# Twenty node tiles of layer 3 kept in SBUF for layer 4, and seven subtractions of the prologue moved to GpSimd

## The chip, the cores and the metric

The kernel runs on one core of one Trainium2 chip. The metric is the device time of one execution in microseconds (us). A core has TensorE (PE, matrix products), VectorE (DVE), ScalarE (ACT), GpSimd (POOL) and SyncE (SP), and 16 DMA engines that carry transfers between HBM and SBUF for all of them. Each engine works through its own queue in order. A DMA is started by an instruction in the queue of SP, ACT or POOL; rows that are picked by an index list ("gathers") are started by POOL.

## The reference, cut to what matters

A four-layer graph network over 6250 nodes with 256 features and 100,000 edges, sorted by destination. With `h = relu(layernorm(x))`:

```python
msum = segment_sum(h[src], dst)                       # layer 1: mean
h = h @ W1_self + (msum / clip(deg, 1)) @ W1_neigh + b1
hp = relu(h @ W2_pool + b2_pool)                      # layer 2: max
h = h @ W2_self + segment_max(hp[src], dst) @ W2_neigh + b2
h = ((segment_sum(h[src], dst) + h) / (deg + 1)) @ W3_neigh + b3   # layer 3
h = h @ W4_self + (segment_sum(h[src], dst) / clip(deg, 1)) @ W4_neigh + b4
out = x + (h @ W_fc + b_fc)                           # layer 4 and the end
```

Destinations are drawn as `6250 * u**2`, so low node numbers have many incoming edges and high ones few.

## The kernel before, in words

**Tiles.** The nodes are cut into 49 tiles of 128 (NT = 49). A table of rows in HBM holds what a layer needs of every node: `tab_h` in layer 1, `tab_r` in layer 3, `tab_s` in layer 4. Weight products are folded together, so that a node's row in `tab_s` is 256 numbers for the neighbours' sum of layer 4, kept as a high and a low part (2 x 256 fp32r, 2 KB a row, 256 KB a tile), while the node's own part goes to the table `xq`.

**Two ways to sum over neighbours.** For the low node tiles (8 in layer 1, H3 = 20 in layer 3, H4 = 22 in layer 4) the sum is dense: a matrix of edge counts, held in `tab_a` as fp8, times the rows of all 49 tiles, one PE instruction for each pair of a destination and a source tile (function `dense`). For the other node tiles the function `sums` walks over the edges, 128 at a time: POOL gathers 128 rows into one of `deep` slots of `ring` (14 in layer 4), DVE makes a one-hot matrix `hot`, PE multiplies them, and DVE adds the product to `acc`. The dense products stand in a list, the `Hub`; `sums` works it off beside the gathers, so many of the list at each step that the list ends 8 steps before the gathers in layer 4. PE's order in layers 3 and 4 is thus: the products in front of the first step, then one product of a gather and some four dense ones, in turn.

**Layer 3's end of a node tile.** `done3` (lines 1834 to 1868) turns an accumulator into `q`, splits its second half with `halves` (ACT copies the high part, DVE subtracts for the low part) into `q2`, and SP stores `q2` to `tab_s` and the first half to `xq`. For the 20 dense tiles a first part of the sum, made during layer 2, is added: it lies in the 20 tiles `acc3_0` to `acc3_19` of 2 KB a partition, in the pool `span3`, which closes with layer 3. For tiles 33 to 42 (`z4_kept`) `q2` is not a passing buffer: it lies in `zt33` and `zt38` of the pool `zk`, which lives through layer 4.

**Layer 4** (lines 1870 to 1940). It has 22 x 49 = 1078 dense products, 266 gathers and 266 products of gathers. The source tiles come in the order of `order`: first the ten kept ones, then six groups of `z4_late`, which `resident` loads back from `tab_s` on SP's queue. For the first four destination tiles the products go group by group, so that 4 x 10 = 40 of them need no load; `hub.advance(4 * nk)` puts these 40 ahead of the first gather's step. The count matrices come in pieces `ac` on ACT's queue, nine pieces ahead, and ACT widens each to `af`. The working pool `fl4` lies where layer 3's pool `fl3` was. `done4` and `finish4` load x (`xr`) and `xq` (`q`) on ACT's queue, add the sums on DVE, and store `out` on SP's queue.

**The prologue** (lines 660 to 1108). The x rows come in 17 groups of three tiles (the last has one). For each group DVE takes mean and variance (L706 to L714), ACT the root (L715), DVE the inverse and the shift `nb` (L721, L729), ACT normalizes (L731) and casts the high part to bf16 in `Z1` (L733), DVE subtracts it (`middle`, L737), POOL casts the middle part (L739), DVE subtracts again for the lowest part (`lowest`, L743), and SP stores the group to `tab_h` (L745). DVE's order is written out by hand: `lowest` of group g-1 stands inside the statistics of group g+2. A planner orders the other engines, save where `keep_in_program_order` pins an instruction behind the one traced before it on its engine. Five buffers `xt` hold the groups; the load of group g+4 is written behind `lowest` of group g-1, whose buffer it takes, and stands behind its store in SP's queue. POOL also issues five gathers (`begins`, L806) in groups 0 and 1 and two (`window_gathers`, L872) in each of groups 5 to 12.

Of the kernel before, what the change touches and what calls it, by code (L numbers as in the profile page):

```python
# [9 lines left out]
F32 = mybir.dt.float32  # L10
# [3 lines left out]
F32R = mybir.dt.float32r  # L14
# [7 lines left out]
P = 128  # L22
# [56 lines left out]
def fast_path(  # L79
# [15 lines left out]
    nc = tc.nc  # L95
    N, FI = x.shape
    E = src.shape[0]
    FH = W1_self.shape[1]
    FO = W_fc.shape[1]
    NT = (N + P - 1) // P  # L100
# [7 lines left out]
    LG = 7  # L108
# [7 lines left out]
    for d in range(NT):  # L116
        m, s = _edges_below(d * P, E, N)
        m1, s1 = _edges_below((d + 1) * P, E, N)
# [9 lines left out]
    for d in range(NT):  # L128
        m, s = _edges_below(d * P, E, N)
        m1, s1 = _edges_below((d + 1) * P, E, N)  # L130
# [7 lines left out]
    H1, H3, H4 = HUB  # L138
# [502 lines left out]
    Z1 = zpool.tile([P, NT, 3 * FI + 4], BF16, name="Z1")  # L641
# [21 lines left out]
    with ExitStack() as pro:  # L663
# [6 lines left out]
        xts = []  # L670
# [69 lines left out]

        def lowest(g):
            i0, LG = groups[g]
            nc.vector.tensor_sub(Z1[:, i0 : i0 + LG, 2 * FI : 3 * FI], xts[g],  # L743
                                 Z1[:, i0 : i0 + LG, FI : 2 * FI])
            nc.sync.dma_start(  # L745
                tab_h[i0 * P : (i0 + LG) * P, :].rearrange("(c p) f -> p c f", p=P),
                Z1[:, i0 : i0 + LG, :],
            )
# [110 lines left out]
        nk = max(RB1, RB * P - RB1)  # L859
# [239 lines left out]
    with ExitStack() as on:  # L1099
# [91 lines left out]
        hub = Hub(made.rest() + work)  # L1191
# [105 lines left out]
    nc.scalar.dma_start(srcE, stash_e[0, :, jb - JC * P : T - JC * P].bitcast(I32))  # L1297
    keyE = span4.tile([P, T - jb], F32, name="keyE")
    nc.scalar.dma_start(keyE, stash_e[1, :, jb - JC * P : T - JC * P])
    acc3 = [span3.tile([P, FH], F32, name=f"acc3_{d}") for d in range(H3)]  # L1300
    begun = set()

    def add3(d, v):
# [517 lines left out]
    with ExitStack() as on:  # L1821
        psd = on.enter_context(tc.tile_pool(name="psd3", bufs=2, space=PSUM))
        psg = on.enter_context(tc.tile_pool(name="psg3", bufs=3, space=PSUM))
        psm = on.enter_context(tc.tile_pool(name="psm3", bufs=2, space=PSUM))
        one_tag[id(psm)] = "pm"
        zk = on.enter_context(tc.tile_pool(name="fz4", bufs=1, side="right"))
        Z4 = {}
        z4_kept = ((33, 38), (38, 43))
        z4_late = ((0, 7), (7, 14), (14, 20), (20, 27), (27, 33), (43, NT))
        for s0, s1 in z4_kept:  # L1830
            zt = zk.tile([P, s1 - s0, 2 * FO], F32R, name=f"zt{s0}", bufs=1)
            Z4.update({s: zt[:, s - s0, :] for s in range(s0, s1)})

        with tc.tile_pool(name="fl3", bufs=2) as wk:
            def done3(d, acc):
                q = wk.tile([P, FH], F32, name="q", bufs=2)
                if d < H3:
                    nc.vector.tensor_add(q, acc, acc3[d])
                    nc.vector.scalar_tensor_tensor(q, q, rgcn[:, d : d + 1], qrow,
                                                   op0=ALU.mult, op1=ALU.add)  # L1840
                else:
                    if d in Z3:
                        z = Z3[d]
                    else:
                        z = wk.tile([P, 3 * FH], BF16, name="zown", bufs=1)
                        with tc.issue_after(kept_stores[-1].ins):
                            nc.sync.dma_start(z, tab_r[d * P : (d + 1) * P, :])
                        yield 1
                        yield 1
                        yield 1  # L1850
                    if d < NT - 4:
                        for part in range(3):
                            nc.vector.tensor_add(acc, acc, z[:, part * FH : (part + 1) * FH])
                            yield 1
                    else:
                        own = bank(psm, "pm", "pm_own")
                        for part in range(3):
                            nc.tensor.matmul(own, ident_b, z[:, part * FH : (part + 1) * FH],
                                             start=(part == 0), stop=(part == 2))
                        yield 1  # L1860
                        nc.vector.tensor_add(acc, acc, own)
                    nc.vector.scalar_tensor_tensor(q, acc, rgcn[:, d : d + 1], qrow,
                                                   op0=ALU.mult, op1=ALU.add)
                q2 = Z4[d] if d in Z4 else wk.tile([P, 2 * FO], F32R, name="q2")
                halves(q[:, FO:], FO, q2)
                nc.sync.dma_start(tab_s[d * P : (d + 1) * P, :], q2.bitcast(F32))
                nc.sync.dma_start(xq[d * P : (d + 1) * P, :], q[:, :FO])
                yield 1

            late = ((0, 4), (4, KEPT), (EARLY[1], 45), (45, NT))  # L1870
            Z3 = {s: kept_rows[0][:, s, :] for s in range(KEPT)}
            with tc.issue_after(kept_stores[-1].ins):
                for s0, s1 in ((EARLY[1], NT),):
                    Z3.update(resident(wk, tab_r, FH, s0, s1))
            block = stream(wk, [(d, s0, s1) for d in range(H3) for s0, s1 in late], wk,
                           lambda s: s < KEPT)
            todo = []
            work = []
            for d in range(H3):
                work += dense([s for s0, s1 in late for s in range(s0, s1)], lambda s, d=d: block(d, s), lambda s: Z3[s], FH, psd,  # L1880
                              lambda acc, d=d: todo.append(done3(d, acc)), own=d,
                              halved=range(KEPT))
            sums(wk, psg, tab_r, FH, srcE, keyE, jb, H3, done3, 11, Hub(work), wait=14, todo=todo,
                 rest=12)

        upto3.close()
        settle(zk, on.enter_context(tc.tile_pool(name="flp", bufs=1, space=PSUM)))
        with tc.tile_pool(name="fl4", bufs=2) as wk:
            loaded4 = {}

            def load4(d):
                n = P if d < NFULL else NREM
                xr = wk.tile([P, FI], F32, name="xr4", bufs=10)
                nc.scalar.dma_start(xr[:n, :], x[d * P : d * P + n, :])
                q = wk.tile([P, FO], F32, name="q4", bufs=10)
                nc.scalar.dma_start(q[:n, :], xq[d * P : d * P + n, :])
                loaded4[d] = n, xr, q

            def done4(d, acc):
                for i in range(d, min(d + 3, H4 if d < H4 else NT)):  # L1900
                    if i not in loaded4:
                        load4(i)
                return finish4(d, acc)

            def finish4(d, acc):
                n, xr, q = loaded4.pop(d)
                yield 1
                yield 1
                yield 1
                nc.vector.tensor_add(xr[:n, :], xr[:n, :], q[:n, :])  # L1910
                for c in range(0, acc.shape[1], FO):
                    nc.vector.scalar_tensor_tensor(xr[:n, :], acc[:n, c : c + FO],
                                                   rmean[:n, d : d + 1], xr[:n, :],
                                                   op0=ALU.mult, op1=ALU.add)
                nc.sync.dma_start(out[d * P : d * P + n, :], xr[:n, :])

            order = [*z4_kept, *z4_late]
            first = range(4)
            block = stream(zk, [(d, *c) for c in order for d in first]
                           + [(d, *c) for d in range(4, H4) for c in order],  # L1920
                           wk, deep=9, ahead=4)
            todo = []
            parts4 = []
            for d in range(H4):
                parts4.append(dense([s for s0, s1 in order for s in range(s0, s1)],
                                    lambda s, d=d: block(d, s), lambda s: Z4[s], FO, (psd, psm)[d // 2 % 2],
                                    lambda acc, d=d: todo.append(done4(d, acc)), wide=True))
            nk = sum(s1 - s0 for s0, s1 in z4_kept)
            cuts = [sum(s1 - s0 for s0, s1 in order[:i]) for i in range(len(order) + 1)]
            hub = Hub([w for a, b in zip(cuts, cuts[1:]) for d in first for w in parts4[d][a:b]]  # L1930
                      + [w for p in parts4[4:] for w in p])
            hub.advance(4 * nk)
            for s0, s1 in z4_late:
                Z4.update(resident(wk, tab_s, FO, s0, s1))
            sums(wk, psg, tab_s, FO, srcE, keyE, jb, H4, done4, 14, hub, wait=4, todo=todo,
                 rest=8, wide=True)
# [643 lines left out]
```

## Time and profile before

| what | value |
|---|---|
| median of 3 runs | 2724.58 us (2719.38 to 2725.16) |
| the profiled execution | 2732.06 us, its span 2730.3 us |
| prologue, to the first gather of layer 1 | to about 113 us |
| layer 3 | about 1960 to 2360 us |
| layer 4, from its first product to the end | 2360.8 us to the end |
| busy over the span: PE, DVE, POOL, ACT | 84%, 76%, 68%, 48% |

The profile comes from one execution. A timeline row gives start and duration in us, engine (SPq and ACTq are queues that issue DMAs), line, operation, and in square brackets how long the engine was idle before, and what ended that. A row of stretches gives the stretch, its length, the busy time of each engine with the number of its instructions, the granted TensorE clock as a share of full speed, the mean busy share of the 16 DMA engines, and what they moved in GB/s.

### The profile page before, as it was taken

The page shows a single profiled execution, that of the slowest core. Times are in us where ns is not written, and L with a number is a line of the kernel's source. Part 1 is how long each engine was busy: PE and PEld are TensorE (multiplying, and loading weights), DVE is VectorE, ACT ScalarE, POOL GpSimd, SP SyncE. Part 2 cuts the span into 40 slices and gives each one's busy share as a digit, 9 for nine tenths or more (in the row PEclk, how much of TensorE's full clock was granted, in tenths as well). Part 3 has the DMA queues.
Part 4 walks back from the last instruction along what each step waited for, and adds up shares of the span by engine and source line. Part 5 has one row for each costly group of instructions (what it writes and reads, how often), then busy time and mean ns, then how long its engine had stood idle before and what let it go on. Part 6 is the DMA issues. An engine that isn't in the chain of part 4 may idle for free.

```text
span 2730.3 us, 37722 instructions
## 1 busy us (share of the span) xinstructions
PE 2303.3 (84%) x10402; PEld 1436.1 (53%) x10402; DVE 2084.6 (76%) x5540; ACT 1301.6 (48%) x2859; POOL 1858.7 (68%) x2169
## 2 busy tenths in 40 slices
PE   4688999999787366566978999898799999879987
PEld 2356666777443132222645666655345445568766
DVE  8888777776489898888678998888467777557666
ACT  4467777764278888696422333232211111234443
POOL 5477777777567677677656676566477777667775
PEclk8799999999898578778989999999899999989999
DMA  8567777777699899899989999999799999999996
GB/s 272 157 178 206 209 206 212 217 222 232 200 356 341 295 343 346 290 322 358 342 288 305 339 343 318 283 321 311 283 380 385 378 383 363 333 364 351 315 302 216
DMA packets 365625, 809.90 MB, mean 297 GB/s; under 512 B 56238, under 2 KB 154646, under 8 KB 365372
## 3 DMA queue, kind: packets, MB, share of 16 engines
q0 software_dynamic: 143248, 501.86, 56.3%
q1 hardware_dynamic: 145928, 215.57, 21.7%
q10 hardware_dynamic: 76228, 89.96, 9.7%
q8 instruction: 85, 1.39, 0.2%
q14 instruction: 136, 1.11, 0.1%
HBM read 602.51 MB, written 205.46 MB: 296 GB/s over the span
## 4 chain that ended last, share of the span: by engine, by line
PE 49%; DMA 26%; DVE 13%; issue 5%; ACT 2%; POOL 2%; ACTq 0%; DVEq 0%; POOLq 0%; SPq 0%
PE pd L574 18%; PE pg L513 11%; DMA X<-rows,srcIf 9%; DMA ring<-tab_h,srcT 4%; DVE run L1669 3%; PE pm_hp L1175 3%; PE pm_prf L1558 3%; DMA rows<-X 2%; DMA xr<-in_x 2%; PE pm_hp L1169 2%; PE pb L349 2%; DVE acc L544 2%; DVE X L1669 2%; DMA out<-xr 2%; PE pm_prf L1552 2%
## 5 line engine op out<-in xcount | busy, mean ns | idle before, releaser
L1688 POOL DMA_INDIRECT X<-rows,srcIf x782 | 744.5, 952 | 368.0 <-issue 143.8
L1669 DVE SCALAR_TENSOR_TENSOR run<-run,samef,X 128x512 f32<-128x512 f32 x758 | 573.1, 756 | 52.8 <-DMA X<-rows,srcIf 47.1
L492 POOL DMA_INDIRECT ring<-tab_h,srcT x474 | 456.7, 963 | 150.1 <-issue 53.2
L513 PE MATMUL pg<-ring,hot 128*128 128x259 bf16 (+1 forms) x2292 | 475.1, 316 | 45.9 <-DMA ring<-tab_h,srcT 34.8
L544 DVE SCALAR_TENSOR_TENSOR acc<-pg,M,acc 128x256 f32<-128x256 f32 (+2 forms) x617 | 314.6, 536 | 79.5 <-PE pg L513 71.1
L492 POOL DMA_INDIRECT ring<-tab_r,srcE x290 | 292.1, 1007 | 117.1 <-issue 51.8
L1794 ACT CAST af<-ac 128x768 fp32r<-128x768 fp8e4 (+3 forms) x216 | 172.7, 805 | 384.7 <-DMA ac<-tab_a 193.4
L513 PEld LDWEIGHTS <-hot 128*128 128x128 bf16 x2292 | 214.0, 98 | 231.6 <-issue 108.7
L492 POOL DMA_INDIRECT ring<-tab_s,srcE x266 | 255.4, 960 | 110.5 <-PE pg L510 34.8
L566 PE MATMUL pd<-zt,af 128*128 128x512 f32 x1078 | 300.7, 402 | 33.5 <-ACT af L1794 30.5
L1669 DVE SCALAR_TENSOR_TENSOR X<-X,samef,run 128x512 f32<-128x512 f32 x379 | 282.3, 745 | 38.1 <-DMA X<-rows,srcIf 23.1
L574 PE MATMUL pd<-kept_rows,aw 128*128 128x512 f32 x920 | 293.9, 443 | 12.7 <-ACT aw L1624 6.5
L566 PEld LDWEIGHTS pd<-zt,af 128*128 128x128 f32 x1078 | 207.3, 194 | 86.2 <-ACT af L1794 38.9
L574 PEld LDWEIGHTS pd<-kept_rows,aw 128*128 128x128 f32 x920 | 175.8, 194 | 85.1 <-issue 35.3
L488 DVE TENSOR_SCALAR hot<-iota_bf,keyE 128x128 bf16<-128x128 bf16 (+1 forms) x556 | 143.9, 281 | 82.8 <-PE pg L513 51.9
L1558 PE MATMUL pm_prf<-unf,hTf 128*128 128x512 f32 x384 | 201.3, 649 | 1.9 <-ACT hTf L1548 1.3
L341 ACT ACTIVATE hs<-ht,onef 128x128 bf16<-128x128 bf16 x396 | 153.5, 393 | 90.6 <-PE pb L349 89.5
L1624 ACT CAST aw<-ae 128x512 fp32r<-128x512 fp8e4 x160 | 99.2, 621 | 188.0 <-PE pd L574 173.4
L574 PE MATMUL pd<-Z,A 128*128 128x256 bf16 (+1 forms) x1176 | 184.1, 273 | 0.8 <-ACT A L354 0.7
L375 ACT ACTIVATE ht<-iota_bf,skR 128x128 bf16<-128x128 bf16 x448 | 157.9, 402 | 12.8 <-DMA col<-in_L_gnn_b 8.9
L340 ACT ACTIVATE ht<-iota_bf,sk 128x128 bf16<-128x128 bf16 x396 | 153.1, 398 | 8.3
L393 PE MATMUL pb<-hm,hs 128*128 128x196 bf16 x448 | 82.2, 282 | 87.9 <-ACT A L398 77.5
(391 smaller groups left out, 4184.1 us busy)
## 6 DMA issues: line engine op xcount, KB each, us to landing
rows<-X SPq DMA_DIRECT2D x385, 256.0 KB, 4.8
tab_r<-r ACTq DMA_DIRECT2D x48, 384.0 KB, 4.7
rows<-hpf SPq DMA_DIRECT2D x49, 256.0 KB, 3.6
th<-tab_t ACTq DMA_DIRECT2D x49, 256.0 KB, 6.1
X<-rows,srcIf POOLq DMA_INDIRECT x782
tab_a<-A ACTq DMA_DIRECT2D x14, 784.0 KB, 6.6
ae<-tab_a SPq DMA_DIRECT2D x160, 64.0 KB, 4.9
tab_s<-q SPq DMA_DIRECT2D x39, 256.0 KB, 6.9
```

What stands on the lines that cost most here:

```text
L340: nc.scalar.activation(t, iota_b, AF.Abs, bias=sk[:, r : r + 1])
L341: nc.scalar.activation(hots[0], t, AF.Relu, bias=one, scale=-1.0)
L375: nc.scalar.activation(held["ht"][:, i, :], iota_b, AF.Abs, bias=sk[:, r : r + 1])
L492: nc.gpsimd.indirect_dma_start(out=ring[:, j % deep, :].bitcast(F32) if wide else ring[:, j % deep, :], out_offset=None, in_=table, in_off ...
L513: mm = nc.tensor.matmul(pg[:, : F + c], hot[j], X[:, part * F : (part + 1) * F + c], start=(k == 0 and part == 2), stop=(k == n - 1 and pa ...
L544: nc.vector.scalar_tensor_tensor(acc[d], half, m, acc[d], op0=ALU.mult, op1=ALU.add)
L566: nc.tensor.matmul(hold[0], a, z, start=(s == ss[0]), stop=(s == ss[-1]))
L574: nc.tensor.matmul(hold[0][:, : F + c], a, z[:, part * F : (part + 1) * F + c], start=(first and s != own), stop=(s == ss[-1] and part == ...
L1558: nc.tensor.matmul(pm, hT[:, c, :], un[:, c, :], start=False, stop=(c == KH - 1))
L1669: nc.vector.scalar_tensor_tensor(put, held, st, row, op0=ALU.mult, op1=ALU.max)
L1688: nc.gpsimd.indirect_dma_start(out=X[:, k, :], out_offset=None, in_=tab_p, in_offset=bass.IndirectOffsetOnAxis(ap=srcI[:, t : t + 1], axis=0),
L1794: nc.scalar.copy(wide[i][:, :n, :], got[i][:, :n, :])
```

## The change

1. The tiles `acc3_0` to `acc3_19` move from the pool `span3` to `span4`, which lives through layer 4. When `done3` of a dense tile d has read `acc3_d`, its `q2` is written to a new tile in the same place, `z4_d`. It is still stored to `tab_s`, since gathers read any row.
2. In layer 4 the source order starts with tiles 0 to 19, then the ten kept ones, then those that are loaded: 20 to 26, 27 to 32 and 43 to 48. Three loads (tiles 0 to 19) are gone, and 4 x 20 = 80 products instead of 40 stand ahead of the first gather's step.
3. In the prologue `lowest` of the odd groups 1 to 13 (seven of 17) runs on POOL; all 17 are pinned in program order. On POOL each stands behind the cast and the gathers of its own group and ahead of the cast of the next.

```diff
         def lowest(g):
             i0, LG = groups[g]
-            nc.vector.tensor_sub(Z1[:, i0 : i0 + LG, 2 * FI : 3 * FI], xts[g],
-                                 Z1[:, i0 : i0 + LG, FI : 2 * FI])
+            by = nc.gpsimd if g % 2 and g < 14 else nc.vector
+            tc.keep_in_program_order(
+                by.tensor_sub(Z1[:, i0 : i0 + LG, 2 * FI : 3 * FI], xts[g],
+                              Z1[:, i0 : i0 + LG, FI : 2 * FI]))
...
-    acc3 = [span3.tile([P, FH], F32, name=f"acc3_{d}") for d in range(H3)]
+    acc3 = [span4.tile([P, FH], F32, tag=f"acc3_{d}", name=f"acc3_{d}", bufs=1) for d in range(H3)]
...
+        z4_first = ((0, 7), (7, 14), (14, H3))
         z4_kept = ((33, 38), (38, 43))
-        z4_late = ((0, 7), (7, 14), (14, 20), (20, 27), (27, 33), (43, NT))
+        z4_late = ((H3, 27), (27, 33), (43, NT))
...
+                if d < H3:
+                    Z4[d] = span4.tile([P, 2 * FO], F32R, tag=f"acc3_{d}", name=f"z4_{d}", bufs=1)
                 q2 = Z4[d] if d in Z4 else wk.tile([P, 2 * FO], F32R, name="q2")
...
-            order = [*z4_kept, *z4_late]
+            order = [*z4_first, *z4_kept, *z4_late]
...
-            nk = sum(s1 - s0 for s0, s1 in z4_kept)
...
-            hub.advance(4 * nk)
+            hub.advance(4 * H3)
```

## The prediction, made before the changed kernel was run

> **What bounds the kernel now.** I read the stretches first, then the chain of waits, then the timelines of PE and POOL where layer 4 starts, and the same for the prologue. The change touches only these two places, so only they are priced. Stretches of layer 4 (columns: stretch, length, PE, PEld, DVE, ACT, POOL busy with counts, PE clock, DMA share, GB/s):
>
> ```profile
> 2360.00:2380.00 20.00, 19.16 (x73) 15.19 (x74) 6.22 (x24) 10.85 (x14) 14.60 (x16) 0.86 0.95 348
> 2380.00:2400.00 20.00, 13.36 (x51) 10.32 (x50) 4.76 (x14) 4.36 (x5) 15.12 (x17) 0.91 1.04 409
> 2400.00:2420.00 20.00, 8.57 (x28) 6.00 (x28) 3.20 (x10) 2.94 (x4) 6.22 (x7) 0.67 1.04 390
> 2450.00:2500.00 50.00, 50.00 (x221) 41.23 (x220) 37.37 (x119) 23.65 (x29) 38.12 (x40) 1.00 1.02 354
> 2600.00:2650.00 50.00, 42.92 (x174) 33.10 (x175) 30.25 (x94) 20.33 (x24) 38.03 (x40) 0.97 0.93 301
> ```
>
> In steady work PE does 221 products in 50 us, 0.226 us each. From 2380 to 2420 it does 79, where 177 would fit: PE starves for 22 us, its clock falls to 0.67, and the DMA engines are full. The chain says on what:
>
> ```profile
> 2375.13 33.04 DMA zt<-tab_s
> ```
>
> These are the reloads of layer 3's rows, which the change halves. The last PE hole ends at 2418.09, behind them; PE's first 40 products, of the kept tiles, had taken 11.8 us:
>
> ```profile
> 2360.84 11.80 PE L566 MATMUL pd<-zt,af 128*128 128x512 f32 x40 [5.63 <-ACT af L1794]
> ...
> 2418.09 1.22 PE L566 MATMUL pd<-zt,af 128*128 128x512 f32 x2 [8.80 <-ACT af L1794]
> ```
>
> But PE's holes are not yet the kernel's loss. The gathers on POOL are a second pacer: one every 1.25 us, 266 of them. In the timeline of POOL, and in the view of all instructions on `tab_s`:
>
> ```profile
> 2360.83 0.94 POOL L492 DMA_INDIRECT ring<-tab_s,srcE  x1 [13.47 <-DVE hot L488]
> 2362.08 0.95 POOL L492 DMA_INDIRECT ring<-tab_s,srcE  x1 [0.30 <-issue]
> ...
> 2408.71 0.94 POOL L492 DMA_INDIRECT ring<-tab_s,srcE  x1 [1.91 <-PE pg L510]
> 2420.01 0.94 POOL L492 DMA_INDIRECT ring<-tab_s,srcE  x1 [10.36 <-PE pg L510]
> 2422.14 0.94 POOL L492 DMA_INDIRECT ring<-tab_s,srcE  x1 [1.19 <-PE pg L510]
> 2424.24 0.94 POOL L492 DMA_INDIRECT ring<-tab_s,srcE  x1 [1.16 <-PE pg L510]
> ```
>
> ```profile
> L492 POOL DMA_INDIRECT ring<-tab_s,srcE x266: 940/946/1265, 2360.8 to 2712.3; - x133
> ```
>
> From first to last issue are 351.5 us over 265 intervals; at 1.25 us they would be 331.3. So POOL lost 20.2 us in all. Of these, 14.62 - 4 x 0.30 = 13.4 us lie in the four waits shown, where the 14 ring slots were full since PE stood still; the other 6.8 us are spread over the rest. A dense product more or less costs nothing while POOL paces: a step holds one gather's product and on average 1038/254 = 4.09 dense ones, 5.09 x 0.226 = 1.15 us, under 1.25.
>
> **Layer 4, edit by edit.** Removed: three of six reloads, 20 tiles x 256 KB = 5.1 MB of 10.0 MB. The store to `tab_s` stays, all 49 of them; where `q2` lies costs nothing, since ACT and DVE write it as before and `acc3_d` has been read by the addition just ahead, on the same DVE. Moved: 80 products instead of 40 stand ahead of the first gather's step, and the list behind them shrinks to 998/254 = 3.93 a step, 4.93 x 0.226 = 1.11 us. The layer cannot start sooner: the first gather needs the last row of `tab_s`.
>
> What the move costs: 40 products took 11.8 us, the next 40 at 0.226 take 9.0, so the first gather's product ends at about 2360.84 + 20.8 + 0.4 = 2382.0. POOL can be 14 gathers ahead; its 15th would go at 2360.83 + 14 x 1.25 = 2378.3, so it stands still for 3.7 us. That is a new wait; behind it in POOL's queue are only more gathers, and PE has 14 of them landed.
>
> Do the three reloads that stay come in time? The first reload's landing, by the view of DMA issues, took
>
> ```profile
> zt<-tab_s SPq DMA_DIRECT2D x3, 1792.0 KB, 24.0
> ```
>
> from its issue, so about 2384; the six were through when PE resumed at 2418, so (2418 - 2384)/5 = 7 us for each later one, and the three are there at about 2384, 2391 and 2398. PE needs them after 80 and 40 products: 40/3.93 = 10 steps of 1.11 behind 2382 is 2393, then 28 products on, 2401, and 24 more, 2408. Each has at least 9 us of slack, so the 13.4 us go. What is late next is the gather itself.
>
> Sum of layer 4: -13.4 + 3.7 = -9.7 us; the other 6.8 us of POOL stay, and the tail behind the last gather is the same. Bounds: if the 6.8 go too, because PE is no longer behind, -16.5. At the other end all 80 products run as slowly as those of the stretch 2400 to 2420, 8.57/28 = 0.306 us, which holds POOL until 2385.7, for 7.4 us; and the three reloads that stay stop PE half as long as the six did, 6.7 us: -13.4 + 7.4 + 6.7 = +0.7. I take -9.7, by the row of the 40 and by the slack of the reloads.
>
> **The prologue.** Groups of instructions up to 190 us, then rows of DVE, POOL and SP:
>
> ```profile
> L743 DVE TENSOR_TENSOR Z<-xt,Z 128x768 bf16<-128x768 f32 x16 | 14.9, 929 | 1.3 <-POOL Z L739 1.3
> ...
> L739 POOL CAST Z<-xt 128x768 bf16<-128x768 f32 x16 | 13.8, 866 | 41.9 <-DVE xt L737 35.8 <-ACT xt L731 5.1 <-DVE atF L834 0.5
> ```
>
> ```profile
> 35.35 0.43 DVE L706 BATCH_NORM_STATS2 st<-xt 128x6 f32<-128x256 f32 x1 [1.49 <-DMA xt<-in_x]
> ...
> 42.39 0.43 DVE L706 BATCH_NORM_STATS2 st<-xt 128x6 f32<-128x256 f32 x1 [1.37 <-DMA xt<-in_x]
> ...
> 60.56 0.85 DVE L881 TENSOR_SCALAR wrowf<-wrow,atF 128x128 f32<-128x128 int32 x1
> ...
> 65.49 0.28 DVE L881 TENSOR_SCALAR wrowf<-wrow,atF 128x128 f32<-128x128 int32 x1
> ...
> 75.90 0.18 DVE L721 RECIPROCAL rs<-sd 128x3 f32<-128x3 f32 x1 [2.33 <-ACT sd L715]
> ```
>
> ```profile
> 25.23 0.95 POOL L806 DMA_INDIRECT Wb<-dflat,cI  x1 [0.30 <-issue]
> ...
> 60.51 0.83 POOL L739 CAST Z<-xt 128x768 bf16<-128x768 f32 x1 [0.47 <-DVE atF L834]
> ...
> 65.71 0.88 POOL L739 CAST Z<-xt 128x768 bf16<-128x768 f32 x1 [2.00 <-DVE xt L737]
> ...
> 69.54 0.88 POOL L739 CAST Z<-xt 128x768 bf16<-128x768 f32 x1 [0.47 <-ACT sd L715]
> ```
>
> ```profile
> 24.59 0.49 SPq L681 DMA_DIRECT2D xt<-in_x  x1
> ```
>
> Removed from DVE: 7 x 0.93 = 6.5 us. The price on POOL is not in the trace: no two-input operation runs there. From below it is the cast, 0.87 us (one operand read); from above twice that, 1.73, since it reads two. I take 1.73: with one operand POOL is at 0.87 where DVE with two is at 0.93, so nothing in these rows lets a second operand through for nothing. The Trainium skill ("GPSIMD Engine Reference", Performance versus the Vector engine) measures an elementwise addition of two operands at 1.96 times DVE's time and speaks against such a move; by it an estimate is 1.96 x 0.93 = 1.82 us, and the prologue would come out 0.4 us worse than below. No run here shows it yet.
>
> Group 1: its subtraction queues behind the gather that ends at 26.18, and ends at about 28.0. The load of group 6 stands behind its store on SP, so it goes at 28.4, not 24.59: 3.8 us late, and it was this load that DVE awaited at 35.35. DVE waits at 42.39 for another load, which is not late; so 1.37 us of the delay are absorbed there, and 0.93 us by the saving of group 3: +1.5. Groups 5 to 12: POOL has two gathers a group, casts follow each other by 3.83 us (65.71 to 69.54) and only 0.47 of that is idle. A pair of groups takes 7.66, with the subtraction 7.66 - 0.94 + 1.73 = 8.45: POOL becomes the pacer by 0.8 us for each of the last two pairs, and 2.33 us of DVE's wait for ACT at 75.90 hide one of them: +0.8. In the first two pairs the casts come later (2.00 idle), but a POOL operation stops DVE: the same L881 takes 0.85 us beside a cast (60.56 to 61.41, the cast ends at 61.34) and 0.28 without one. Of a subtraction's 1.73 us I let half fall on such work, 0.87, which eats the 0.93 saved: 0. Group 13 has an idle POOL: -0.9. Sum of the prologue: 1.5 + 0.8 - 0.9 = +1.4 us, passed on whole, since DVE has no idle time left there to absorb it, by the stretch (columns as above):
>
> ```profile
> 100.00:115.00 15.00, 6.92 (x23) 2.67 (x22) 14.79 (x70) 3.37 (x10) 3.28 (x4) 0.57 0.47 168
> ```
>
> Bounds: -6.5 if nothing of it comes back; +7 if the load is 3.8 us late with nothing absorbed and all four pairs lose 0.8.
>
> **Sum.** -9.7 + 1.4 = -8.3 us. The profiled execution took 2732.06 us (span 2730.3), 7.5 above the median of 2724.58; it would take 2723.8, and the median of the runs 2716.3.
>
> **Rivals.** (a) More than that: the 6.8 us go as well, PE being ahead of the gathers and not behind, and the prologue is even: -16.5, 2708. For it: with PE's work at 1.11 us a step there is slack of 0.14 a step. Against: part of the 6.8 us are long POOL instructions (up to 1265 ns).
>
> (b) Hidden: the gain at 2420 is given back where DVE waits for x,
>
> ```profile
> DVE xr L1910 <- DMA xr<-in_x: 19.0, 4, 6.2
> ```
>
> 19 us in the stretch 2600 to 2650, in which PE does 174 products instead of 221. If these waits pace the second half, the end moves by the prologue alone: 2726. For it: the chain runs through these loads. Against: POOL issues its 40 gathers in that stretch nonetheless, 38.03/0.95, so its early lead is kept.
>
> (c) Slower: the subtraction on POOL is dearer than two casts. All seven lie on the prologue's path then, 7 x (X - 0.93); against -9.7 it decides, by +5.4 and more, from X = 0.93 + 15.1/7 = 3.1 us. At 3.3 us the time is 2724.6 - 9.7 + 16.6 = 2731.5. For it: POOL's cast is already no faster than DVE with two operands, and the output is a mix of f32 and bf16. Against: 3.1 is 3.6 times the cast.
>
> **How the numbers follow.** This kernel's runs spread by 5.8 us, about 0.2% (5.4 us), which is what can be told from no change: faster is below 2719.1, slower above 2730.0. The forecast, -5.4 to -14, has 0.50; (a) 0.18; (b), and all between, 0.22; (c) 0.10. So faster 0.68, same 0.22, slower 0.10. The likeliest is 2716, its own range 2711 to 2719; over both signs 2705 to 2728, which leaves out the far end of (a) and (c).
>
> **What would show it.** In the profile after: POOL's idle time for PE in 2405 to 2425 gone, one wait of about 4 us near 2378 to 2382 in its place (less the shift of the whole); 80 products in a row at the start of layer 4, about 21 us; three reloads and no PE hole over 2 us before 2420; 266 gathers in some 342 us. In the prologue seven L743 on POOL of about 1.7 us, longer DVE rows beside them, the load of group 6 behind 28 us, and the first gather of layer 1 about 1.4 us later than before. The prediction is wrong if the reloads still stop PE, if POOL's lost time in layer 4 stays near 20 us, or if the subtraction takes over 3 us.

## The result, and the profile after

The changed kernel takes 2718.39 us, median of 20 runs (2714.48 to 2728.29), against 2726.75 us for the kernel before (20 runs). The ratio is 0.9967, with a 95% interval from 0.9955 to 0.9978: by the ratio 9.0 us less (6.0 to 12.3), while the two medians differ by 8.4. 2716 was predicted. The profiled execution took 2719.89 us, its span 2718.1.

Only the two places that the change touches have moved. From the first gather of layer 1 to the first of layer 4 there are 2248.1 us in both profiles. The first gather of layer 1 goes at 115.0 us instead of 112.7; layer 4 takes 2718.1 - 2363.1 = 355.0 us from its first gather to the end, instead of 369.5.

Layer 4 in stretches counted from its first gather (columns: stretch, length, busy time with number of instructions of PE, PEld, DVE, ACT, POOL, PE clock, DMA share, GB/s). After:

```profile
2363.00:2383.00 20.00, 19.72 (x75) 16.05 (x76) 1.30 (x7) 9.54 (x12) 13.28 (x14) 0.85 0.98 371
2383.00:2403.00 20.00, 18.71 (x82) 14.91 (x81) 7.57 (x27) 11.42 (x16) 13.83 (x15) 1.00 1.03 376
2403.00:2423.00 20.00, 20.00 (x89) 16.54 (x89) 17.34 (x54) 9.95 (x12) 15.12 (x17) 1.00 1.03 359
2423.00:2463.00 40.00, 39.86 (x175) 32.42 (x174) 30.77 (x95) 18.87 (x24) 30.55 (x32) 1.00 1.02 361
2463.00:2563.00 100.00, 94.28 (x393) 71.10 (x392) 65.43 (x203) 40.47 (x49) 75.91 (x80) 1.00 0.96 323
2563.00:2663.00 100.00, 87.78 (x366) 66.61 (x365) 60.87 (x190) 38.48 (x47) 75.90 (x80) 1.00 0.92 302
```

The same stretches of the kernel before:

```profile
2360.80:2380.80 20.00, 19.96 (x76) 15.82 (x77) 5.66 (x21) 10.12 (x13) 15.13 (x16) 0.88 0.99 365
2380.80:2400.80 20.00, 13.36 (x52) 10.31 (x51) 4.54 (x13) 4.36 (x5) 15.13 (x16) 0.91 1.04 409
2400.80:2420.80 20.00, 8.57 (x26) 6.00 (x25) 3.20 (x10) 3.64 (x4) 6.47 (x7) 0.65 1.04 387
2420.80:2460.80 40.00, 40.00 (x171) 32.80 (x170) 32.12 (x99) 20.31 (x25) 28.96 (x31) 0.96 1.00 341
```

PE does 82 + 89 products from 20 to 60 us, where it did 52 + 26, and from 20 us on the clock stays at 1.00. By these rows POOL has issued 14 + 15 + 17 + 32 = 78 gathers after 100 us instead of 70. A row counts a gather that runs over a border in both stretches; counted by their starts they are 76 and 69, so seven more, of 1.25 us each: 8.8 us. From there on it issues 80 in each 100 us (79 and 80 before), so what was won is kept. The rows at the start of layer 4 after the change, from the timelines of PE and POOL and the view of all instructions on `tab_s`:

```profile
2363.28 21.13 PE L566 MATMUL pd<-z,af 128*128 128x512 f32 x80 [5.84 <-ACT af L1796]
2386.82 1.20 PE L566 MATMUL pd<-zt,af 128*128 128x512 f32 x4 [1.29 <-ACT af L1796]
```

```profile
2384.90 0.94 POOL L492 DMA_INDIRECT ring<-tab_s,srcE  x1 [4.61 <-PE pg L510]
```

```profile
L492 POOL DMA_INDIRECT ring<-tab_s,srcE x266: 942/949/1292, 2363.1 to 2702.8; - x133
```

The 80 products took 21.1 us (20.8 were said), one PE hole of 1.29 us is left in the first 60 us, POOL's one wait is 4.61 us, 4.3 over its usual 0.30, and the 266 gathers take 339.7 us.

In the prologue, the groups of instructions up to 190 us:

```profile
L739 POOL CAST Z<-xt 128x768 bf16<-128x768 f32 x16 | 13.6, 848 | 31.3 <-DVE xt L737 30.3 <-ACT Z L733 1.0
L745 POOL TENSOR_TENSOR Z<-xt,Z 128x768 bf16<-128x768 f32 x7 | 11.6, 1651 | 0.3
L745 DVE TENSOR_TENSOR Z<-xt,Z 128x768 bf16<-128x768 f32 x9 | 8.4, 933 | 1.4 <-POOL Z L739 1.4
```

A subtraction takes POOL 1.65 us, 1.78 times DVE's 0.93. What DVE does meanwhile, first POOL's rows, then DVE's:

```profile
33.12 1.64 POOL L745 TENSOR_TENSOR Z<-xt,Z 128x768 bf16<-128x768 f32 x1
47.35 1.65 POOL L745 TENSOR_TENSOR Z<-xt,Z 128x768 bf16<-128x768 f32 x1
...
68.00 1.66 POOL L745 TENSOR_TENSOR Z<-xt,Z 128x768 bf16<-128x768 f32 x1
```

```profile
33.13 1.65 DVE L818 SCALAR_TENSOR_TENSOR SN<-cF,within 128x1 f32<-128x1 f32 x1
...
47.38 1.65 DVE L714 TENSOR_SCALAR sd<-mv 128x3 f32<-128x3 f32 x1
...
67.29 0.17 DVE L714 TENSOR_SCALAR sd<-mv 128x3 f32<-128x3 f32 x1
67.36 3.12 DVE L737 TENSOR_TENSOR xt<-xt,Z 128x768 f32<-128x768 f32 x1
```

The same L714 on three numbers a partition takes 0.17 us alone and 1.65 us beside POOL's subtraction; L737 takes 0.95 us alone. DVE stands for the whole of POOL's instruction. Of the seven, five lengthen a DVE operation by 1.3 to 2.2 us and a sixth by 0.7; the seventh (78.00) falls where DVE is idle. The statistics keep their time: an L706 that began at 26.86, just ahead of POOL's subtraction at 26.91, took 0.39 us, and the L729 behind it 2.17 instead of 0.14.

### The profile page after: what moved, and what is told of

Same layout as the page of the kernel before. It is cut to its first block, busy times and chain, and to the rows that moved or that the text cites. A ratio compares the mean times of both kernels' runs of the same rounds, so it can differ in the third digit from the quotient of the medians.

```text
span 2718.1 us, 37693 instructions
## 1 busy us (share of the span) xinstructions
PE 2308.2 (85%) x10402; PEld 1432.7 (53%) x10402; DVE 2089.8 (77%) x5533; ACT 1299.4 (48%) x2859; POOL 1873.7 (69%) x2176
## 4 chain that ended last, share of the span: by engine, by line
PE 52%; DMA 22%; DVE 13%; issue 5%; ACT 4%; POOL 3%; ACTq 0%; DVEq 0%; SPq 0%; POOLq 0%
PE pd L574 18%; PE pg L513 11%; DMA X<-rows,srcIf 5%; DMA ring<-tab_h,srcT 3%; PE pm_prf L1560 3%; DVE run L1671 3%; PE pm_hp L1177 3%; PE pd L566 3%; PE pm_prf L1554 3%; DMA xr<-in_x 2%; DMA th<-tab_t 2%; DMA rows<-X 2%; PE pm_hp L1171 2%; PE pb L349 2%; POOL X L1690 2%
## 5 line engine op out<-in xcount | busy, mean ns | idle before, releaser
L1796 ACT CAST af<-ac 128x896 fp32r<-128x896 fp8e4 (+3 forms) x216 | 171.7, 805 | 371.9 <-DMA ac<-tab_a 161.9
L492 POOL DMA_INDIRECT ring<-tab_s,srcE x266 | 255.6, 961 | 98.6 <-issue 28.4
L566 PE MATMUL pd<-zt,af 128*128 128x512 f32 x638 | 176.2, 392 | 7.0 <-ACT af L1796 7.0
L488 DVE TENSOR_SCALAR hot<-iota_bf,keyT 128x128 bf16<-128x128 bf16 x474 | 123.2, 269 | 40.1 <-PE pg L513 38.7
```

What stands on the lines that cost most here:

```text
L488: nc.vector.tensor_scalar(hot[j], iota_b, keyT[:, j - jb : j - jb + 1], None, op0=ALU.is_equal)
L492: nc.gpsimd.indirect_dma_start(out=ring[:, j % deep, :].bitcast(F32) if wide else ring[:, j % deep, :], out_offset=None, in_=table, in_off ...
L566: nc.tensor.matmul(hold[0], a, z, start=(s == ss[0]), stop=(s == ss[-1]))
L1796: nc.scalar.copy(wide[i][:, :n, :], got[i][:, :n, :])
```

## The parts alone

Two theories: the two parts lie one behind the other, each passed on whole (1); or the prologue's delay is made up later or was chance (2).

**Only the rows kept** (`lowest` as in the kernel before, the rest of the change as it is):

> Only the rows stay in SBUF; all 17 subtractions are on DVE again. Theory 1 (the two parts lie one behind the other, and each is passed on whole): the first gather of layer 1 goes at 112.7 us instead of the changed kernel's 115.0, layer 4 takes from first to last gather 340 us as in the changed kernel, and the time is 9.0 + 2.3 = 11.3 us below the kernel before. Theory 2 (the 2.3 us of the prologue are made up later, or are chance): 9.0 us below, like the changed kernel.

Measured: 2714.46 us, ratio 0.9937 (0.9916 to 0.9958), 17.2 us below before (11.5 to 22.9). The first gather of layer 1 went at 109.5 us, layer 4 took 357.0 us.

**Only the seven subtractions on GpSimd** (layers 3 and 4 as in the kernel before):

> Only the seven subtractions move to GpSimd; layer 4 is that of the kernel before. Theory 1: first gather of layer 1 at 115.0 us, time 2.3 us above the kernel before. Theory 2: 0, the delay is absorbed between layer 1 and layer 4 or was not there. If the trade on GpSimd paid, as my lower bound allowed, it would be up to 6.5 us below.

Measured: 2732.91 us, ratio 1.0015 (0.9998 to 1.0031): 4.1 us above before, with an interval from -0.5 to +8.5. First gather of layer 1 at 115.1 us, layer 4 in 367.7 us.

Both parts go the way of theory 1, and further than it said (17.2 for 11.3, 4.1 for 2.3), but a single time does not settle a few us. The traces do it better. From layer 1's first gather to layer 4's the work is the same in every kernel here, yet it took between 2239.9 and 2253.3 us in eleven profiles (all but the three of the runs at about 3150 us; that it was 2248.1 in both of the first two is chance); so only what lies ahead of it and behind it is compared. With all subtractions on DVE, the first gather went at 112.7, 109.5, 112.1, 111.1, 109.6 and 109.8 us in six profiles (mean 110.8); with seven on GpSimd at 115.0 and 115.1. So the subtractions cost 4.2 us, known to about 1 us, since six profiles of the same prologue differ by 3.2. Layer 4, first gather to end, took 369.5 and 367.7 us with the old layer 4 (mean 368.6), and 355.0, 357.0, 354.0, 354.3 and 356.7 us with the new one in five profiles (mean 355.4; two of them from e1_rows_only and the changed kernel, three from kernels of the section on the prologue; kernels with another layer 4 are left out). So the rows save 13.2 us. Together that is -9.0, which is what the runs of the changed kernel show.

## What the 13.2 us in layer 4 are

**56 products ahead instead of 80**, so that POOL does not wait at its 15th gather:

```diff
-            hub.advance(4 * H3)
+            hub.advance(4 * 14)
```

> As e1_rows_only, with 56 products instead of 80 ahead of the first gather's step: PE is through with them 24 x 0.23 = 5.5 us sooner, so the wait of POOL for PE at its 15th gather (4.3 us in the changed kernel) goes. Theory 1 (POOL's gathers pace layer 4): 4.3 us less than e1_rows_only, so 15.6 below before. Theory 2 (PE paces in the mean, the wait is only moved; or the waits for x take the gain back): within 1 us of e1_rows_only, and POOL waits for PE or DVE waits for xr that much longer further on.

Measured: 2719.16 us, ratio 0.9955 (0.9934 to 0.9975), 12.3 us below before; not better than e1_rows_only. The wait at the 15th gather is gone, and PE has a hole instead. Rows of PE and of ACT:

```profile
2396.66 1.65 PE L566 MATMUL pd<-zt,af 128*128 128x512 f32 x3 [6.96 <-ACT af L1794]
```

```profile
2395.88 0.72 ACT L1794 CAST af<-ac 128x640 fp32r<-128x640 fp8e4 x1 [8.60 <-DMA ac<-tab_a]
```

Theory 2 of that expectation holds: the wait is only moved. After 100 us POOL has issued 78 gathers by the rows of stretches, no more than in the changed kernel. Further on its profile is worse: POOL waits for PE again, once for 4.9 us, and layer 4 takes 364.5 us against 357.0 in e1_rows_only. That execution was the slowest of its nine (2729.53 us), so how usual this is stays open. And PE's hole (an idle time of PE) does not end with a reloaded row: it ends when the count matrices (`ac`, widened to `af`) are there. That was not in my account, in which PE waited for the rows.

**The rows kept, and the same bytes loaded nevertheless:**

```diff
             for s0, s1 in z4_late:
                 Z4.update(resident(wk, tab_s, FO, s0, s1))
+            for s0 in range(0, H3, 5):
+                spare = wk.tile([P, 5, 2 * FO], F32R, name="spare", bufs=1)
+                nc.sync.dma_start(spare.bitcast(F32),
+                                  tab_s[s0 * P : (s0 + 5) * P, :].rearrange("(c p) f -> p c f", p=P))
```

> As e1_rows_only, and tiles 0 to 19 of tab_s are loaded all the same behind the three reloads, 5.1 MB in four pieces into a buffer that nobody reads. Theory 1 (the gain is PE not waiting for rows): within 2 us of e1_rows_only, 9 to 11 us below before. Theory 3 (the gain is the traffic taken away: the 16 DMA engines were full from 2380 to 2420, and 5.1 MB at 350 GB/s are 14.6 us): the gathers land later, POOL waits 10 us or more for PE again, and the time is 0 to 2 us below before.

Measured: 2735.55 us, ratio 1.0018 (1.0003 to 1.0033): the whole gain is gone and somewhat more, although no product needs what is loaded. Layer 4 takes 376.3 us, 19.3 more than in e1_rows_only. Its stretches:

```profile
2356.50:2376.50 20.00, 19.73 (x79) 16.19 (x80) 1.31 (x7) 9.54 (x12) 13.24 (x14) 0.90 1.00 372
2376.50:2396.50 20.00, 13.11 (x48) 9.73 (x47) 2.52 (x9) 6.65 (x9) 11.33 (x12) 0.87 1.05 400
2396.50:2416.50 20.00, 18.53 (x77) 14.41 (x75) 6.05 (x21) 5.87 (x7) 14.48 (x15) 0.96 1.02 374
2416.50:2456.50 40.00, 33.18 (x132) 26.87 (x133) 31.44 (x98) 19.10 (x23) 24.02 (x24) 0.87 0.97 332
```

After 100 us POOL has issued 65 gathers, fewer than the 70 of before. So the gain is the loads that are not made, not the rows that are at hand. Why the same 5.24 MB cost 19.3 us here and no more than 13.2 in the kernel before is not shown; the four extra loads share one buffer, so each is issued when the one before has landed, and they run on for longer. The view of the DMA queues says who gives way (q1 is SP's queue, the reloads; q10 is ACT's, counts and x; q0 the gathers; columns: packets, MB, share of the DMA engines). Over 20 us in the kernel before, from 2382 us, and in the changed kernel, from 2384 us:

```profile
DMA packets 3794, 8.19 MB, mean 409 GB/s; under 512 B 389, under 2 KB 1189, under 8 KB 3792
q0 software_dynamic: 1311, 4.30, 53.0%
q1 hardware_dynamic: 1585, 3.18, 41.0%
q10 hardware_dynamic: 896, 0.68, 10.1%
```

```profile
q0 software_dynamic: 1091, 3.56, 46.8%
q10 hardware_dynamic: 3488, 2.60, 39.2%
q1 hardware_dynamic: 648, 1.29, 16.8%
```

At its steady rate PE does 178 dense products in 50 us (2450 to 2500 us, the other products being those of gathers), each with a count block of 16 KB: 1.2 MB in 20 us. The kernel before got 0.68 MB for counts and x together while the reloads took 3.18; the changed kernel got 2.60. ACT had issued 12 transfers in the one stretch and 29 in the other. The DMA engines are full in both. The three loads that are gone are 20 x 0.262 = 5.24 MB; at the 8.19 MB that the kernel before moved in those 20 us (409 GB/s) that is 12.8 us, against 13.2 measured. The run with the extra loads shows that this is no fixed price: there the same bytes cost 19.3 us.

**The kernel before with its reloads in small pieces.** The counts can be kept from PE in two ways: the engines have no room for them, or ACT cannot issue them. The second is there too. SP's and ACT's DMAs take turns on eight completion semaphores (counters that show that a transfer has landed; numbers 100 and 102 to 108 in the trace), and an issue waits until the semaphore's last transfer has landed. In the trace of before, ACT's issue of a count load at 2384.6 us waits for the semaphore of the reload issued at 2360.5, the one at 2394.8 for that of the reload issued at 2371.4, and the one at 2416.7 for that of the reload issued at 2408.2. ACT stands for 8.5, 7.4 and 9.2 us ahead of these issues, 25.1 in all; behind them in its queue are the casts to `af`. The view of waits for 2360 to 2430 us shows two of the three under this name:

```profile
ACT af L1794 <- DMA zt<-tab_s: 19.2, 2, 10.9
```

In the changed kernel these holds are 8.2 and 1.0 us. In e4_extra_loads they are 30 us in five, three of them behind the extra loads, so that run does not tell the two ways apart.

To do that, each reload was cut into one DMA per tile, in the kernel before, and in the kernels with 56 and 80 products ahead:

```diff
-                Z4.update(resident(wk, tab_s, FO, s0, s1))
+                zt = wk.tile([P, s1 - s0, 2 * FO], F32R, name=f"zt{s0}", bufs=1)
+                for s in range(s0, s1):
+                    nc.sync.dma_start(zt[:, s - s0, :].bitcast(F32), tab_s[s * P : (s + 1) * P, :])
+                    Z4[s] = zt[:, s - s0, :]
```

> The kernel before, with each of the six reloads of layer 4 cut into one DMA per node tile: 39 of 256 KB instead of six of 1.5 to 1.8 MB, same bytes, same queue. In the trace of before, the DMAs of SP and ACT take turns on eight completion semaphores, and ACT's issue of a count load waits at 2384.6, 2394.8 and 2416.7 us for a semaphore that a reload holds until it has landed, 24, 23 and 8 us after its issue; ACT's later casts to af, and PE behind them, stand still for that time. Theory S (this hold of ACT's queue is what starves PE): with small pieces no hold is longer than some 3 us, PE does 140 products or more from 20 to 60 us behind the start of layer 4 instead of 79, and the time is 8 to 14 us below before. Theory R (PE lacks the rows themselves) and theory T (the traffic): the same 10 MB have to come, and the time is within 3 us of before.

> As e3_ahead56 (rows kept, 56 products ahead of the first gather), with the three reloads cut into one DMA per node tile. Theory S: the PE hole of 7.0 us behind the 56 products goes, since it was ACT's wait for a reload's semaphore; no PE hole above 2 us, POOL waits less than 1 us for PE at its 15th gather, and the time is 3 to 5 us below e1_rows_only. Theory T: the counts come late through the traffic of the same 4.9 MB, the hole stays at 5 us or more, and the time is that of e3_ahead56.

> As e1_rows_only (80 products ahead), with the three reloads cut into one DMA per node tile. Theory S: the 80 products already cover ACT's wait, so the time is within 3 us of e1_rows_only; POOL's wait of 3.9 us at its 15th gather stays.

When these three ran, the kernel before itself took 3148.85 us, with 1.47 us from gather to gather in layer 4, so they are set only against each other and against it: ratios 1.0008 (0.9981 to 1.0035), 0.9992 (0.9968 to 1.0017) and 0.9997 (0.9974 to 1.0019). None of the three differs from before there, not even the one with the rows kept and 80 products ahead. Whether that is the pieces or the slower pace of the gathers is open, since e1_rows_only was not run beside them. The first was run once more, when the kernel before took 2729.61 us:

> The same kernel as f1_before_pieces (the kernel before, its six reloads cut into 39 DMAs of 256 KB). That run fell on a chip on which every kernel took 3149 us, with 1.47 us from gather to gather of layer 4 instead of 1.25 and waits of the engines for nothing that the trace shows; there PE's holes of 8.8 us and POOL's waits of 10.4 us had shrunk to 1.9 and 3.1 us, but the time cannot be set against the 2730 us of the kernel before elsewhere. Still open is what the pieces are worth where a gather comes every 1.25 us. Theory S: PE does 140 products or more from 20 to 60 us behind the start of layer 4 instead of 79, POOL loses 8 to 12 us less, and the time is 8 to 14 us below before. Theories R and T: within 3 us of before.

Measured: 2728.93 us, ratio 0.9998 (0.9980 to 1.0016), no gain. Its second and third stretch, and ACT's row:

```profile
2383.10:2403.10 20.00, 13.61 (x49) 9.33 (x47) 4.60 (x13) 3.41 (x4) 15.14 (x16) 0.91 1.04 407
2403.10:2423.10 20.00, 13.94 (x48) 9.96 (x48) 3.21 (x10) 5.55 (x8) 9.54 (x11) 0.83 1.03 376
```

```profile
2390.65 0.94 ACT L1794 CAST af<-ac 128x896 fp32r<-128x896 fp8e4 x1 [9.42 <-DMA zt<-tab_s]
```

PE does 97 products from 20 to 60 us, 19 more than before and far from the 140 that theory S asked for; in the next 40 us it does 146 instead of 171. POOL stands at 71 gathers after 100 us, and the time is the same. The pieces did only half of what they were made for: ACT stands behind them for 13.7 us in all (five holds of 1 us and more) instead of 25.1, but one wait of 9.42 us is still there, since with the DMA engines full a piece of 256 KB takes up to 10.9 us to land. So theory S in its form (large loads, long holds) is refuted, and that half of the holds went without any gain speaks for the bytes. It does not prove it: which of the two, room on the engines or ACT's turn on a semaphore, keeps the counts back at a given moment stays open.

**x loaded earlier.** Rival (b) was that the gain is given back at DVE's waits for x in the second half. In e1_rows_only these waits are 73.5 us:

```diff
-                for i in range(d, min(d + 3, H4 if d < H4 else NT)):
+                for i in range(d, min(d + 6, H4 if d < H4 else NT)):
```

> As e1_rows_only, with done4 loading x and xq six node tiles ahead instead of three. In the profile of e1_rows_only DVE waits 73.5 us in 24 waits for xr in layer 4, and 17.1 us pass from the last gather to the end. Theory B (these waits take back part of the gain: PE falls behind the gathers in the second half, so that some 10 of 14 ring slots are full at the end instead of 3 or 4): the waits shrink below 25 us, the end comes 7 x 1.1 = 8 us sooner after the last gather, and the time is 5 to 8 us below e1_rows_only. Theory 1 (POOL paces throughout): within 2 us of e1_rows_only.

Measured: 2717.23 us, ratio 0.9958 (0.9942 to 0.9974), 11.5 us below before; no better than e1_rows_only. DVE's waits in the view from 2430 us on:

```profile
DVE xr L1913 <- DMA xr<-in_x: 82.6, 27, 5.1
```

They did not shrink: ACT's queue issues the x of a tile none or one tile ahead of its use from 2465 us on, in e1_rows_only and here, wherever the load is written. One reason is in the trace of e1_rows_only: at 2481.8 and 2532.3 us ACT's issue of an x stood 4.7 and 3.4 us for the semaphore of a store of `out`. The edit missed its aim, so what these waits cost is open. That the changed kernel keeps its lead is shown by its 80 gathers in each 100 us.

## What the 4.2 us in the prologue are

Three kernels, each run once and read by the first gather of layer 1 in its profile. All have the new layer 4. Group 1 left on DVE, so that the load of group 6 is not late:

```diff
-            by = nc.gpsimd if g % 2 and g < 14 else nc.vector
+            by = nc.gpsimd if g % 2 and 1 < g < 14 else nc.vector
```

> The changed kernel, with group 1's subtraction left on DVE, so six on GpSimd. First gather of layer 1: 109.5, 112.7, 112.1 and 111.1 us in the four profiles with all subtractions on DVE, 115.0 and 115.1 with seven on GpSimd. Theory L (the late load of group 6 is the main cost, my +1.5): 113.5 us or sooner, and no wait of DVE for that load. Theory H (GpSimd holds DVE for the whole of its subtraction, 1.65 us, against 0.93 saved, 0.72 a piece): 114.3 us.

All 17 on DVE, and seven more of the same size on GpSimd that nobody waits for:

```diff
-            by = nc.gpsimd if g % 2 and g < 14 else nc.vector
+            by = nc.vector
...
+            if g % 2 and g < 14:
+                tc.keep_in_program_order(
+                    nc.gpsimd.tensor_sub(Z1[:, i0 + LG : i0 + 2 * LG, 2 * FI : 3 * FI], Z1[:, i0 : i0 + LG, :FI],
+                                         Z1[:, i0 : i0 + LG, FI : 2 * FI]))
```

> All 17 subtractions on DVE as before, and GpSimd does seven more of the same size in the odd groups 1 to 13, on other operands, whose results are overwritten; no store or load waits for them. Theory H (the hold): each stops DVE for about 1.65 us with nothing saved, 7 x 1.65 = 11.6 us less the 2.3 us that DVE waits for ACT anyway: first gather of layer 1 at 118 to 122 us. Theory L (late loads) or theory Q (GpSimd's own queue paces groups 5 to 12, 0.8 us a pair): 111 to 114.6 us.

All 17 on GpSimd (`by = nc.gpsimd`):

> The changed kernel, with all 17 subtractions on GpSimd. Theory H: (17 - 7) x 0.72 = 7 us later than the changed kernel, first gather of layer 1 at about 122 us. Theory Q: each of the eight groups 5 to 12 takes 3.83 - 0.47 + 1.65 = 5.0 us on GpSimd, 4 x 2 x 1.2 = 9.4 us more in all than before: 121 us, with DVE waiting for GpSimd rather than its rows being long. If the trade were even: 115 us.

Measured, against a mean of 110.8 us with all on DVE (109.5 to 112.7):

| kernel | first gather of layer 1 | above 110.8 | per piece on GpSimd |
|---|---|---|---|
| six on GpSimd (group 1 on DVE) | 114.8 | 4.0 | 0.67 |
| seven (the changed kernel) | 115.0 | 4.2 | 0.60 |
| 17, of which 16 full size | 121.2 | 10.4 | 0.65 |
| seven extra, nothing saved on DVE | 118.4 | 7.6 | 1.09 |

The group-1 run gives back 0.2 us, not 1.5: theory L falls. The extra subtractions cost 7.6 us although DVE waits for no load and not for them; all of DVE's waits from 20 to 112 us in that kernel:

```profile
DVE srcT L932 <- PE pt_e L928: 0.4, 1, 0.4
```

So it is the hold: theory H. In that kernel DVE is busy for 96.4 us from 20 us to the first gather, against 85.0 in the kernel before and 84.5 in e1_rows_only: 11.4 to 11.9 us more, which is seven holds of 1.65 us whole. The delay is smaller than that, since DVE's idle time in this stretch shrinks from 7.7 and 5.0 us to 2.0. Where DVE saves its own 0.93 us, the price is 0.6 to 0.67 us a piece (0.72 expected), with an error of some 0.1 to 0.3 from the scatter between profiles. That it is the same for 16 pieces is in part chance: in the run with 17 DVE also waits, 6.7 us for x and 2.5 for GpSimd.

The Trainium skill ("SBUF — State Buffer", SBUF: two separate sides) says that VectorE and GpSimd share a pair of ports as an exclusive lock: whichever starts first has it for the whole instruction, and the other fully blocks; on VectorE's side it names instructions in a 2-port mode and those with two inputs in SBUF. The rows above agree as to the whole instruction, 1.65 us for an operation of 0.17; in which mode that L714 ran, no row shows.

## Why the prediction came out as it did

The sum was -8.3 us; measured are -9.0. That closeness is in part luck: layer 4 gained 3.5 us more than said and the prologue lost 2.8 us more.

- **Where POOL loses time.** The 13.4 us of four waits went, as said. The new wait was 4.3 us instead of 3.7. But e3_ahead56 shows that taking this wait away wins nothing: POOL starts 17 gathers in the first 20 us instead of 14, the third reload lands 31.1 us after its issue instead of 26.0, PE's counts come late, and after 100 us POOL is where it was. That the earlier gathers take the DMA time is the likely reason, not a shown one. "The other 6.8 us of POOL stay" failed: POOL lost 339.7 - 331.3 = 8.4 us in all, so 4.1 besides the wait, and 2.7 of the 6.8 went. "The tail is the same" was off too: 17.8 us on average with the old layer 4 (18.0 and 17.5), 16.1 with the new one.
- **Why the reloads cost.** The step "PE starves ... on these reloads", with the slack worked out for each reload's rows, named the wrong link for most of the loss. Of PE's four holes of more than 2 us in the kernel before only the first, 2.96 us, ends with a reload's rows; the other three, 15.1 us with the one that the prediction showed, end with a cast of counts:

```profile
2384.69 0.47 PE L566 MATMUL pd<-zt,af 128*128 128x512 f32 x1 [2.96 <-DMA zt<-tab_s]
2396.57 1.22 PE L566 MATMUL pd<-zt,af 128*128 128x512 f32 x2 [3.68 <-ACT af L1794]
2406.28 1.73 PE L566 MATMUL pd<-zt,af 128*128 128x512 f32 x4 [2.63 <-ACT af L1794]
```

e4_extra_loads shows the loss coming back with no row missing. What the reloads take is DMA time and ACT's turns on the semaphores, and the counts on ACT's queue are what PE then lacks. Priced by bytes, the removal is worth 12.8 us. That number stood in the prediction's rows (20 tiles of 256 KB; 409 GB/s with the DMA engines full), and was not worked out; the 19.3 us of e4_extra_loads show that its closeness to 13.2 is in part luck too.
- **When the reloads land.** The row with 24.0 us is a median of three loads, and was read as the first one's time. The first landed after 11.2 us, the last of the six at 2420.5. In the changed kernel the three are there at 2373.3, 2384.9 and 2389.3 us (2384, 2391 and 2398 were said), so the slack was there, and larger.
- **The subtraction on POOL.** 1.65 us, just under the upper bound of 1.73 that I took; rival (c), from 3.1 us on, is out. The ratio that the Trainium skill ("GPSIMD Engine Reference", Performance versus the Vector engine) gives for an addition, 1.96, is 1.78 here for the subtraction, so the estimate of 1.82 us worked out from it was too high.
- **The load of group 6.** It went at 29.04 us (28.4 said). "+1.5" failed all the same: DVE's waits for x from 20 to 112 us are 0.9 us in all, and p1_group1_on_dve gives back 0.2. All of DVE's waits in that stretch, after:

```profile
DVE xt L678 <- POOL Z L745: 2.5, 1, 2.5
DVE st L706 <- DMA xt<-in_x: 0.9, 1, 0.9
```

- **GpSimd as the pacer of groups 5 to 12, +0.8.** The one wait for POOL that shows is the first of these rows, 2.5 us for the subtraction at 78.00 us, in the place of the 2.33 us for ACT.
- **The hold.** "Of a subtraction's 1.73 us I let half fall on such work" is the term that was mis-sized. Five of seven stop DVE for 1.3 us or more; 1.65 - 0.93 = 0.72 a piece makes 5.0 us, and 4.2 were measured. p3_extra_subs shows the hold by itself.

Rival (a), whose layer 4 is -16.5, is as far from the 13.2 us on one side (3.3) as the forecast on the other (3.5), and part of what it said came true: some of the 6.8 us went. Rival (b) did not come about in the changed kernel.

The rows alone are then likely the better change: e1_rows_only stands at 0.9937 (0.9916 to 0.9958) and the changed kernel at 0.9967 (0.9955 to 0.9978). The intervals overlap a little, and the two other kernels with the rows and no moved subtraction stand between (0.9955 and 0.9958); but the first gather of layer 1 (115.0 us against a mean of 110.8) points the same way.

## What to carry to other kernels

Where the DMA engines are full, price a transfer that goes by its bytes over the rate of that stretch, as a first estimate (12.8 us for 13.2 here, but the same bytes put back in another place cost 19.3), not by the one wait in which the loss shows; a wait that is taken away there can turn up elsewhere. Find out which transfer gives way by the bytes per queue: it can be one that the change does not touch. Work that is moved from VectorE to GpSimd must be set against the whole of GpSimd's duration on VectorE, unless what runs beside it is seen to keep its time.

## What the runs showed that was not expected

- A DVE operation of 0.17 us takes 1.65 us beside GpSimd's subtraction, and seven such subtractions that nobody waits for delay the prologue by 7.6 us. On two bf16 operands (p3_extra_subs) a subtraction takes 1.64 to 1.66 us as well, one of the seven 1.93.
- SP's and ACT's DMAs share eight completion semaphores, so ACT's issue of 0.1 MB stood for 7 to 9 us behind SP's loads of 1.6 to 1.8 MB, and its casts with it.
- When queues compete for full DMA engines, ACT's counts came off worst: 896 packets and 0.68 MB in 20 us beside 1585 packets and 3.18 MB of the reloads. How much of its smaller number of packets is ACT's waiting to issue, no run here shows. By the rows a packet of ACT's queue is 0.76 KB and one of the reloads 2.0 KB. The Trainium skill ("DMA: Bandwidth & Descriptors", Queues, rings and completion order) says that each DMA engine takes turns between the queues it has work for, a whole packet at a time, typically of some 9 to 17 descriptors. Whether the packets counted here are these, no run shows; with equal turns ACT's smaller ones would get fewer bytes.
